# A hybrid of convolution, attention, experts and scans: some scan inputs made by GpSimd, later sums, finer ticks, and the spread in two row groups

## Chip, cores and metric

The kernel runs on one core of a Trainium2 chip, as one program with one launch. The metric is device time in microseconds (us) of a whole execution; lower is better. The engines are TensorE (PE), VectorE (DVE), ScalarE (ACT), GpSimd (POOL) and SyncE (SP), which here issues nearly all DMAs.[...]

## The reference, cut to what matters

Four images of 32 x 32 positions with 256 channels go through four layers. Layer 0 has a state-space scan with 64 states over 512 channels; layer 1 is a grouped convolution block; layer 2 is masked attention and a mixture of 8 experts; layer 3 is a second scan with 16 states, and another mixture of 8 experts. The two scans are what the change is about:

```python
def step(h, inp):                                  # layer 0, N = 64 states
    xt, dtt, Bt, Ct = inp
    dA = jnp.exp(dtt[:, :, None] * A)
    h = dA * h + (dtt * xt)[:, :, None] * Bt[:, None, :]
    y = jnp.einsum('bdn,bn->bd', h, Ct)
    return (h, y)
...
def scan_step(h, inputs):                          # layer 3, N = 16 states
    x_t, dt_t, B_t, C_t = inputs
    A_bar = jnp.exp(dt_t[..., None] * A)
    B_bar = dt_t[..., None] * B_t[:, None, :]
    h_new = A_bar * h + B_bar * x_t[..., None]
    y_t = (h_new * C_t[:, None, :]).sum(axis=-1)
    return (h_new, y_t)
```

There are 1024 time steps for each of 512 channels and 4 images. The mixtures compute, for each expert, `gelu(x @ W1) @ W2` for all tokens, and weight it by the router's value (hidden width 256 in layer 2, 512 in layer 3).

## The kernel before

**Units.** The partitions of a scan hold (channel, state) pairs: 2 channels with 64 states in layer 0, 8 channels with 16 states in layer 3. One such block of 128 x 1024 (float32) is a *unit*. A scan, written (layer, image), has 256 units in layer 0 and 64 in layer 3: for each of four blocks `d` of 128 channels, `c` and `j` choose 32 channels and `i` the group in them. The eight scans, 1280 units, run in the order `SCANS`: (0,0), (0,1), (3,0), (0,2), (3,1), (0,3), (3,2), (3,3).

**One unit, in `scans`.** `load` broadcasts the step widths dt of its channels from DRAM over the states into a tile dA (five buffers): two DMAs of 256 KB in layer 0, eight of 64 KB in layer 3, all issued by SP. `decay` turns dA in place into exp(A dt) on ScalarE. `first` brings dt*x into PSUM (tile ps_rep, two buffers): the program has stored dt*x as three bfloat16 parts (`parts`), which lie in the tile S as 3 x 32 rows, and a product with a table of zeros and ones (`spread`) of 96 rows sums the parts and spreads each channel over its states; there are two products of 512 columns. VectorE multiplies ps_rep by the row B (`rows0`), then runs the scan `tensor_tensor_scan` from dA and ps_rep into h (five buffers). GpSimd multiplies h by C (`rows1`). `pair` then sums over the states on TensorE for two units together into ps_y; after the last pair of a block ScalarE copies ps_y to yo and SP stores it.

**Order within the loop.** At step k the program issues `chunk(k+12)` (the next rows and S where a block begins), `load(k+4)`, `first(k+1)`, `decay(k+2)`, the product by B of unit k; then side work may follow (a `yield`); then the scan of k, the product by C, and on odd k `pair(k-2)`; then side work again.

**Side work and the pacing clock.** All else is written as generators: `front` (layer 0 up to its scan, ending in `steps`, which makes dt and the parts), `middle` (after the scan of layer 0: `back0`, `layer1`, `attention`, `moe`, then `front3`, again with `steps`), and `last` (after the scan of layer 3: `back3`, `moe`). A piece between two yields is a *tick*. `run` decides at each yield of the scan loop whether a tick follows: `Metered` adds a cost for each operation to a clock per engine (`COST`), and up to `TICKS` ticks are added while no engine's clock is past that of vector; the clocks of the other engines are pulled up to at most `LAG` = 4 us behind vector's. A stage starts only when the scan that it needs is done (`STAGES`); a scan starts only when its inputs are stored, else `need` issues side work until they are.

**Ticks that the change touches.** `pipe` runs a list of items through steps, one step behind the other, and yields once per round. In `heads` (attention) a round is the 4 products of values of one block of keys and the 6 products of scores of the next, with two exps. In `moe` a round of kind "h" makes two hidden blocks of 512 columns (ps_h) and evicts the two of the round before by Gelu on ScalarE; a round of kind "o" makes one ps_e, which VectorE adds to tb.

After the last scan the rest of the side work runs alone, and so does `last` of the last image.

Of the kernel before, what the change touches and what calls it, by code (L numbers as in the profile page):

```python
# [16 lines left out]
P = 128  # L17
# [20 lines left out]
SAFE = 40.0  # L38
AHEAD = 12
# [85 lines left out]
class Hybrid:  # L125
# [41 lines left out]
    def pipe(self, items, *steps, cost=1.0):  # L167

        items = list(items)
        for tick in range(len(items) + len(steps) - 1):  # L170
            for s in reversed(range(len(steps))):
                if 0 <= tick - s < len(items):
                    steps[s](items[tick - s])
            yield cost if tick < len(items) else 0.5
# [126 lines left out]
    def scan_setup(self, stage, psum, name, n):  # L301

        nc, pool = self.nc, self.const
        G = P // n
        units = DI // G
        cols = pool.tile([P, units], F32, name="A_" + name)
        flat = self.a[name].rearrange("(u g) n -> u (g n)", g=G)  # L310
        for k in range(0, units, P):
            m = min(P, units - k)
            raw = stage.tile([m, P], F32, name=f"Ar{k}_" + name)
            nc.sync.dma_start(raw, flat[k : k + m, :])
            ps = psum.tile([P, P], F32, tag="pre", name="ps_A")
            nc.tensor.transpose(ps[:, :m], raw, self.ident[:m, :m])
            nc.scalar.activation(cols[:, k : k + m], ps[:, :m], AF.Exp)
        nc.vector.tensor_scalar(cols, cols, -1.0, None, ALU.mult)
        spread = pool.tile([3 * 32, 32 // G, P], BF16, name="spread_" + name)
        for s in range(3):  # L320
            rows = slice(32 * s, 32 * s + 32)
            nc.vector.tensor_copy(
                spread[rows].rearrange("p i (g n) -> p (i g) n", n=n),
                self.ident[rows, rows].unsqueeze(2).to_broadcast([32, 32, n]),
            )
        mine = stage.tile([P, G], F32, name="mine_" + name)
        nc.vector.tensor_reduce(
            mine, self.ident.rearrange("p (g n) -> p g n", n=n), AX.X, ALU.add
        )
        collect = pool.tile([P, 32 // G, 32], F32, name="collect_" + name)  # L330
        nc.gpsimd.memset(collect, 0.0)
        for i in range(32 // G):
            nc.vector.tensor_copy(collect[:, i, G * i : G * i + G], mine)
        return cols, spread, collect

    def scans(self, mp, psum):
# [16 lines left out]
        state = {}  # L353
        y = None

        def chunk(k):
# [17 lines left out]
            S = mp.tile([3 * 32, 4, L], BF16, tag="S", name="S", bufs=2)  # L374
            for s in range(3):
                nc.sync.dma_start(
                    S[32 * s : 32 * s + 32, :, :],
                    self.mem["parts", *scan, d][s].rearrange("(j p) t -> p j t", p=32),
                )
# [16 lines left out]

        def decay(k):
            if k >= len(units):
                return
# [7 lines left out]
        def first(k):  # L407
# [5 lines left out]
            ps = psum.tile([P, L], F32, tag="x", name="ps_rep", bufs=2)  # L413
            for g in range(2):
                cols = slice(g * 512, (g + 1) * 512)
                nc.tensor.matmul(
                    ps[:, cols], lhsT=spread[:, i, :], rhs=chunks[scan, d][:, 2 * c + j, cols],
                    start=True, stop=True,
# [37 lines left out]
        for k in range(len(units) + 4):  # L456
            chunk(k + AHEAD)
            load(k + 4)
            first(k + 1)
            decay(k + 2)  # L460
            if k < len(units):
                a, inp = state.pop(k)
                B, Cm = rows[units[k][0]]
                nc.vector.tensor_tensor(inp, inp, B, ALU.mult)
            yield
            if k < len(units):
                h = mp.tile([P, L], F32, tag="h", name="h", bufs=5)
# [3 lines left out]
            if k % 2 == 1 and 2 <= k < len(units) + 2:  # L471
                pair(k - 2)
# [27 lines left out]
    def run(self):  # L500
# [9 lines left out]
        with tc.tile_pool(name="scan", bufs=1) as mp, tc.tile_pool(  # L510
# [5 lines left out]
            self.nc = Metered(nc, clock)  # L516
# [20 lines left out]
    def steps(self, fp, key, w, src, chunks, bias, u):  # L537
# [3 lines left out]
        for d in range(DC):  # L541
            self.keep(("dt", *key, d), [P, L])
            self.keep(("parts", *key, d), [3, P, L], BF16)
# [27 lines left out]
        def split(item):  # L571
            d, g = item
            r, _, _, x = got[item]
            nc.sync.dma_start(self.mem["dt", *key, d][:, g * 512 : (g + 1) * 512], r)
            X = fp.tile([P, 3, 512], BF16, tag="parts", name="parts", bufs=3)
# [652 lines left out]
    def heads(self, fp, raw, sums, qT, kT, v, maskT, mT, nh, hp):  # L1228
# [41 lines left out]
        yield from self.pipe(range(TB), scores, values, cost=2.6)  # L1270
# [62 lines left out]
    def moe(self, which, b, tb):  # L1333
# [7 lines left out]
        with tc.tile_pool(name=f"m{which}{b}", bufs=1, side="right") as op:  # L1341
# [69 lines left out]
            def one(item):  # L1411
                kind, e, g, i = item
                we1, we2 = weights[e]
                if kind == "h":
# [4 lines left out]
                    got[item] = two = [self.ps("ps_h") for _ in range(2)]  # L1419
                    for s in range(2):  # L1420
                        f = 2 * i + s
                        self.mm(
                            two[s], lambda k: we1[:, k, f * P : (f + 1) * P], xT, 2,
                            slice(g * 512, (g + 1) * 512),
                        )
# [11 lines left out]
            def two(item):  # L1437
                kind, e, g, i = item
                if kind == "h":
                    for s, ps in enumerate(got.pop(item)):  # L1440
                        f = 2 * i + s
                        nc.scalar.activation(
                            hidden_of[e, g][:, f, :], ps, AF.Gelu,
                            bias=b1[:, e * KH + f : e * KH + f + 1],
                        )
# [11 lines left out]
            for n in range(len(blocks) + 1):  # L1457
                if n < len(blocks):
                    items += [("h", *blocks[n], i) for i in range(KH // 2)]
# [271 lines left out]
```

## Time and profile before

Three runs took 7107.39 us in the median (7104.26 to 7117.05). The profiled execution took 7124.43 us; the span from its first to its last instruction is 7122.6 us, with a mean granted TensorE clock of 0.805.

| engine | busy us | share of the span | instructions |
|---|---|---|---|
| PE | 5418.5 | 76% | 20430 |
| DVE | 5222.7 | 73% | 4477 |
| POOL | 3651.6 | 51% | 1801 |
| ACT | 3283.8 | 46% | 4024 |

The 16 DMA engines were busy 49% of the span and moved 939 MB. Busy times are of instructions that compute; instructions that only issue DMAs are not counted, so that SP has no row, and its state is read from the timeline of its issues and from the list of its waits. A row of groups reads: line, engine, operation, output and inputs with shapes, count, busy time, mean duration in ns, and the idle time just before such instructions with what ended it. Where operations are recorded through `Metered` they all carry line 120, so that they are told apart by their tiles: the product by B is the DVE row `ps_rep<-ps_rep,rows`, the scan `h<-dA,ps_rep`, the product by C the POOL row `h<-h,rows`, the spread the PE row `ps_rep<-S,spread`, the sum `ps_y<-h,collect`. Line 391 is the issue of the loads of dA.

### The profile page before, as it was taken

To read this page: it belongs to the slowest core of one execution; us is meant where nothing else is said; L and a number is where in the kernel's file an instruction comes from. 1 tells how busy PE (TensorE), PEld (TensorE's weight loads), DVE (VectorE), ACT (ScalarE), POOL (GpSimd) and SP (SyncE) were. 2 spreads that over 40 slices of the span, in tenths; PEclk is the share of its full clock that TensorE was granted. 3 is DMA by queue.
4 is the path that set the end of the run, shared out by engine and by line. 5 is a ranking of instruction groups with operands and counts; after the bars stand their busy time and mean duration, and the time that the engine had idled before them with its cause. 6 is when DMAs were issued, how large, how long until landed. Compare 5 with 4: busy or idle time off the path is not lost. (4 is left out here: it accounts for less than half of the span.)

```text
span 7122.6 us, 66100 instructions
## 1 busy us (share of the span) xinstructions
PE 5418.5 (76%) x20430; PEld 2202.8 (31%) x20516; DVE 5222.7 (73%) x4477; ACT 3283.8 (46%) x4024; POOL 3651.6 (51%) x1801
## 2 busy tenths in 40 slices
PE   6185876578897557879689668898598677866979
PEld 2020221032242022234235322243254322523556
DVE  2787898887898986789889877888899830237611
ACT  4164665234457324446547334556375332244411
POOL 1287677665557655555756554556656520045300
PEclk8585876579898577979779778888698788877989
DMA  2356666654456565446656654456666620135421
GB/s 82 82 138 165 159 177 165 173 139 112 118 134 172 162 174 130 114 115 174 175 147 165 175 144 113 115 134 175 164 166 165 161 75 1 48 95 158 117 62 33
DMA packets 395052, 939.02 MB, mean 132 GB/s; under 512 B 83268, under 2 KB 165776, under 8 KB 393040
## 3 DMA queue, kind: packets, MB, share of 16 engines
q1 hardware_dynamic: 392512, 932.10, 49.0%
q8 instruction: 172, 2.82, 0.2%
q0 software_dynamic: 2128, 2.13, 0.2%
q14 instruction: 240, 1.97, 0.1%
HBM read 844.17 MB, written 93.95 MB: 132 GB/s over the span
## 5 line engine op out<-in xcount | busy, mean ns | idle before, releaser
L120 POOL TENSOR_TENSOR h<-h,rows 128x1024 f32<-128x1024 f32 x1280 | 3026.2, 2367 | 2198.5 <-DVE h L120 1876.2
L120 DVE TENSOR_TENSOR_SCAN h<-dA,ps_rep 128x1024 f32<-128x1024 f32 x1280 | 2924.9, 2285 | 250.6 <-issue 98.6
L120 DVE TENSOR_TENSOR ps_rep<-ps_rep,rows 128x1024 f32<-128x1024 f32 x1280 | 1552.0, 1212 | 349.2 <-PE ps_rep L120 326.9
L120 ACT ACTIVATE dA<-dA,A_L_conv_A_log 128x1024 f32<-128x1024 f32 x1024 | 1156.7, 1146 | 853.2 <-DMA dA<-dt 767.9
L120 PE MATMUL ps_rep<-S,spread_L_conv_A_log 96*128 96x512 bf16 x2048 | 766.6, 464 | 893.5 <-DVE h L120 718.8
L120 PE MATMUL ps_y<-h,collect_L_conv_A_log 128*32 128x512 f32 x4096 | 767.4, 766 | 91.6 <-POOL h L120 87.7
L120 PEld LDWEIGHTS <-spread_L_conv_A_log 96*128 96x128 bf16 x2048 | 159.2, 103 | 1696.0 <-DVE h L120 1252.3
L120 PE MATMUL ps_h<-xTm,we 128*128 128x512 f32 x1280 | 594.1, 609 | 9.4 <-ACT h_m L120 9.4
L120 PE MATMUL ps_e<-we,h_m 128*128 128x256 f32 x2560 | 590.1, 382 | 10.5 <-ACT h_m L120 8.7
L120 ACT ACTIVATE p<-ps_sc 128x512 f32<-128x512 f32 x512 | 277.8, 594 | 598.1 <-PE ps_sc L120 429.6
L120 ACT ACT_TABLE_LOAD x356 | 456.7, 1283 | 195.5 <-DMA dA<-dt 123.9
L120 ACT ACTIVATE dA<-dA,A_L_attn_A_log 128x1024 f32<-128x1024 f32 x256 | 293.5, 1148 | 514.8 <-DMA dA<-dt 494.9
L120 PEld LDWEIGHTS ps_e<-we,h_m 128*128 128x128 f32 x2560 | 482.9, 190 | 136.6 <-issue 31.5
L120 PE MATMUL ps_at<-p,v 128*32 128x512 f32 x1024 | 366.8, 638 | 61.8 <-ACT p L120 53.3
L120 PE MATMUL ps_rep<-S,spread_L_attn_A_log 96*128 96x512 bf16 x512 | 190.7, 462 | 279.7 <-DVE h L120 236.5
L120 ACT ACTIVATE h_m<-ps_h,cols 128x512 f32<-128x512 f32 x320 | 209.3, 685 | 279.7 <-PE ps_h L120 278.1
L120 PEld LDWEIGHTS ps_h<-xTm,we 128*128 128x128 f32 x1280 | 246.6, 195 | 294.3 <-issue 243.0
L120 DVE SCALAR_TENSOR_TENSOR tb<-ps_e,cw,tb 128x256 f32<-128x256 f32 x448 | 192.4, 473 | 192.9 <-PE ps_e L120 192.4
L120 PE MATMUL ps_sc<-qT,kT 32*128 32x512 f32 x1024 | 310.1, 682 | 0.0
L120 PE MATMUL ps_at<-p,ones 128*32 128x512 f32 x1024 | 285.5, 638 | 0.0
L120 DVE RECIPROCAL sums<-sums 128x512 f32<-128x512 f32 x16 | 53.6, 3353 | 256.6 <-ACT sums L120 256.6
L120 PEld LDWEIGHTS ps_y<-h,collect_L_conv_A_log 128*32 128x32 f32 x4096 | 98.6, 119 | 448.7 <-issue 217.6
(406 smaller groups left out, 5689.3 us busy)
## 6 DMA issues: line engine op xcount, KB each, us to landing
dA<-dt SPq DMA_DIRECT2D x2048, 256.0 KB
dA<-dt SPq DMA_DIRECT2D x2048, 64.0 KB
we<-in_L_ffn_W_dram SPq DMA_DIRECT2D x64, 512.0 KB
parts<-parts SPq DMA_DIRECT2D x64, 384.0 KB
S<-parts SPq DMA_DIRECT2D x96, 256.0 KB
dt<-sp_r SPq DMA_DIRECT2D x64, 256.0 KB
y<-yo SPq DMA_DIRECT2D x128, 128.0 KB
y_back<-y SPq DMA_DIRECT2D x64, 256.0 KB
```

Source lines behind the costliest of these rows:

```text
L120: return got(*args, **kw)
```

## The change

It has four parts.

1. *Inputs by GpSimd.* `steps` also stores dt*x as float32 (`dtu`). At step k, `early(k+5)` looks at the clocks: if gpsimd's is at least `SPARE` = 2.4 us behind vector's, and none of the two units before is one already, unit k+5 is *given*. Its row dtu is broadcast by SP to a new tile inp (two buffers), as dt is to dA, and gpsimd's clock is put 2.4 us forward. `product` has GpSimd multiply inp by B two units ahead; it calls the bare `self.real` and is not metered again. For a given unit `first` has ScalarE write the exp into ps_rep in place of the spread, `decay` does nothing, VectorE does no product by B, and the scan reads ps_rep as its factor and inp as its input.
2. *Sums two units later.* `pair(k-4)` in place of `pair(k-2)`, and h has seven buffers.
3. *Finer ticks.* In `heads` there is a yield between values and scores; in `moe` a round of kind "h" makes one ps_h.
4. *The spread in two row groups.* S holds, in each quarter of 32 partitions, 3 x 8 rows for one `c` and one half of the time steps, with 8 blocks of 512 columns behind each other; it is filled by 12 DMAs of 64 KB rather than 3 of 256 KB. The table `spread` is repeated in all quarters, and the two products of a unit have 24 rows each, in two different quarters.

The diff, cut to its core:

```diff
+SPARE = 2.4
...
-    def pipe(self, items, *steps, cost=1.0):
+    def pipe(self, items, *steps, cost=1.0, cut=False):
...
                 if 0 <= tick - s < len(items):
                     steps[s](items[tick - s])
+                    if cut and s:
+                        yield cost
...
-        spread = pool.tile([3 * 32, 32 // G, P], BF16, name="spread_" + name)
-        for s in range(3):
-            rows = slice(32 * s, 32 * s + 32)
-            nc.vector.tensor_copy(
-                spread[rows].rearrange("p i (g n) -> p (i g) n", n=n),
-                self.ident[rows, rows].unsqueeze(2).to_broadcast([32, 32, n]),
-            )
+        eighth = stage.tile([P, 8], F32, name="eighth_" + name)
+        nc.vector.tensor_reduce(
+            eighth, self.ident.rearrange("p (a c) -> p c a", c=8), AX.X, ALU.add
+        )
+        spread = pool.tile([P, 8 // G, P], BF16, name="spread_" + name)
+        nc.vector.tensor_copy(
+            spread.rearrange("p i (g n) -> p (i g) n", n=n),
+            eighth.unsqueeze(2).to_broadcast([P, 8, n]),
+        )
...
-            S = mp.tile([3 * 32, 4, L], BF16, tag="S", name="S", bufs=2)
-            for s in range(3):
-                nc.sync.dma_start(
-                    S[32 * s : 32 * s + 32, :, :],
-                    self.mem["parts", *scan, d][s].rearrange("(j p) t -> p j t", p=32),
-                )
+            S = mp.tile([P, 8, 512], BF16, tag="S", name="S", bufs=2)
+            for c in range(2):
+                for g in range(2):
+                    for s in range(3):
+                        at = 32 * (2 * c + g) + 8 * s
+                        nc.sync.dma_start(
+                            S[at : at + 8, :, :],
+                            self.mem["parts", *scan, d][
+                                s, 64 * c : 64 * c + 64, g * 512 : (g + 1) * 512
+                            ].rearrange("(k i) t -> i k t", i=8),
+                        )
...
+        def early(k):
+            late = self.clock["vector"] - self.clock["gpsimd"]
+            if k >= len(units) or late < SPARE or max(given, default=-3) > k - 3:
+                return
+            scan, d, c, i, j = units[k]
+            n = self.states[scan[0]]
+            G = P // n
+            inp = mp.tile([P, L], F32, tag="inp", name="inp", bufs=2)
+            for g in range(G):
+                r = 64 * c + 32 * j + G * i + g
+                nc.sync.dma_start(
+                    inp[g * n : (g + 1) * n, :],
+                    self.mem["dtu", *scan, d][r : r + 1, :].to_broadcast([n, L]),
+                )
+            given[k] = inp
+            self.clock["gpsimd"] += SPARE
+
+        def product(k):
+            if k in given:
+                inp = given[k]
+                self.real.gpsimd.tensor_tensor(inp, inp, rows[units[k][0]][0], ALU.mult)
...
         def decay(k):
-            if k >= len(units):
+            if k >= len(units) or k in given:
                 return
...
+            if k in given:
+                col = (d * P + 64 * c + 32 * j) // G + i
+                nc.scalar.activation(
+                    ps, state[k], AF.Exp, scale=self.tables[scan[0]][0][:, col : col + 1]
+                )
+                state[k] = (ps, given[k])
+                return
             for g in range(2):
-                cols = slice(g * 512, (g + 1) * 512)
+                part = slice(32 * (2 * c + g), 32 * (2 * c + g) + 24)
                 nc.tensor.matmul(
-                    ps[:, cols], lhsT=spread[:, i, :], rhs=chunks[scan, d][:, 2 * c + j, cols],
-                    start=True, stop=True,
+                    ps[:, g * 512 : (g + 1) * 512], lhsT=spread[part, i % (8 // G), :],
+                    rhs=chunks[scan, d][part, 4 * j + G * i // 8, :], start=True, stop=True,
                 )
...
-        for k in range(len(units) + 4):
+        for k in range(len(units) + 6):
             chunk(k + AHEAD)
+            early(k + 5)
             load(k + 4)
+            product(k + 2)
             first(k + 1)
             decay(k + 2)
             if k < len(units):
                 a, inp = state.pop(k)
                 B, Cm = rows[units[k][0]]
-                nc.vector.tensor_tensor(inp, inp, B, ALU.mult)
+                if k not in given:
+                    nc.vector.tensor_tensor(inp, inp, B, ALU.mult)
             yield
             if k < len(units):
-                h = mp.tile([P, L], F32, tag="h", name="h", bufs=5)
+                h = mp.tile([P, L], F32, tag="h", name="h", bufs=7)
...
-            if k % 2 == 1 and 2 <= k < len(units) + 2:
-                pair(k - 2)
+            if k % 2 == 1 and 4 <= k < len(units) + 4:
+                pair(k - 4)
...
-            self.nc = Metered(nc, clock)
+            self.real, self.nc = nc, Metered(nc, clock)
...
+            nc.sync.dma_start(self.mem["dtu", *key, d][:, g * 512 : (g + 1) * 512], x)
...
-        yield from self.pipe(range(TB), scores, values, cost=2.6)
+        yield from self.pipe(range(TB), scores, values, cost=1.3, cut=True)
...
-                    got[item] = two = [self.ps("ps_h") for _ in range(2)]
-                    for s in range(2):
-                        f = 2 * i + s
-                        self.mm(
-                            two[s], lambda k: we1[:, k, f * P : (f + 1) * P], xT, 2,
-                            slice(g * 512, (g + 1) * 512),
-                        )
+                    got[item] = ps = self.ps("ps_h")
+                    self.mm(
+                        ps, lambda k: we1[:, k, i * P : (i + 1) * P], xT, 2,
+                        slice(g * 512, (g + 1) * 512),
+                    )
                     return
...
-                    for s, ps in enumerate(got.pop(item)):
-                        f = 2 * i + s
-                        nc.scalar.activation(
-                            hidden_of[e, g][:, f, :], ps, AF.Gelu,
-                            bias=b1[:, e * KH + f : e * KH + f + 1],
-                        )
+                    nc.scalar.activation(
+                        hidden_of[e, g][:, i, :], got.pop(item), AF.Gelu,
+                        bias=b1[:, e * KH + i : e * KH + i + 1],
+                    )
                     return
...
-                    items += [("h", *blocks[n], i) for i in range(KH // 2)]
+                    items += [("h", *blocks[n], i) for i in range(KH)]
```

More of the change, by code (lines that the diff above doesn't have):

```diff
@@ L352, in scans @@
         chunks, rows = {}, {}
-        state = {}
+        state, given = {}, {}
         y = None
@@ L542, in steps @@
             self.keep(("dt", *key, d), [P, L])
+            self.keep(("dtu", *key, d), [P, L])
             self.keep(("parts", *key, d), [3, P, L], BF16)
```

## The prediction

> **What bounds the kernel now.** I read the page first, then busy time by stretches, then the timeline of two quiet stretches, then the waits. Page: the columns are busy time, share and count; then the 40 slices; then the two costly DVE groups.
>
> ```profile
> PE 5418.5 (76%) x20430; PEld 2202.8 (31%) x20516; DVE 5222.7 (73%) x4477; ACT 3283.8 (46%) x4024; POOL 3651.6 (51%) x1801
> DVE  2787898887898986789889877888899830237611
> POOL 1287677665557655555756554556656520045300
> L120 DVE TENSOR_TENSOR_SCAN h<-dA,ps_rep 128x1024 f32<-128x1024 f32 x1280 | 2924.9, 2285 | 250.6 <-issue 98.6
> L120 DVE TENSOR_TENSOR ps_rep<-ps_rep,rows 128x1024 f32<-128x1024 f32 x1280 | 1552.0, 1212 | 349.2 <-PE ps_rep L120 326.9
> ```
>
> From slice 2 to slice 32 (about 310 to 5800 us) VectorE is at 8 to 9 tenths with two operations per unit. Counting ps_rep operations by stretch puts the scans at: (0,0) 310-1380, (0,1) 1380-2555, (3,0) to 2865, (0,2) to 4005, (3,1) to 4325, (0,3) to 5500, (3,2) to 5810; then no scan until 6330, (3,3) to about 6720, and a tail. So 1024 units of layer 0 take some 4560 us, 4.45 each. Timeline near 1320, where no side work runs (start, duration, instruction, idle before):
>
> ```profile
> 1320.02 2.29 DVE L120 TENSOR_TENSOR_SCAN h<-dA,ps_rep 128x1024 f32<-128x1024 f32 x1 [0.19 <-issue]
> 1322.22 1.21 DVE L120 TENSOR_TENSOR ps_rep<-ps_rep,rows 128x1024 f32<-128x1024 f32 x1
> 1323.61 2.29 DVE L120 TENSOR_TENSOR_SCAN h<-dA,ps_rep 128x1024 f32<-128x1024 f32 x1 [0.19 <-issue]
> ```
>
> A unit is 3.59 us, all VectorE. It is not so in layer 3. The timeline of SP (start, length of the run of issues, count), then that of VectorE:
>
> ```profile
> 6379.25 29.88 SPq L391 DMA_DIRECT2D dA<-dt  x64
> ```
>
> ```profile
> 6397.60 2.29 DVE L120 TENSOR_TENSOR_SCAN h<-dA,ps_rep 128x1024 f32<-128x1024 f32 x1 [0.32 <-DMA dA<-dt]
> 6401.40 2.29 DVE L120 TENSOR_TENSOR_SCAN h<-dA,ps_rep 128x1024 f32<-128x1024 f32 x1 [0.40 <-DMA dA<-dt]
> 6405.13 2.29 DVE L120 TENSOR_TENSOR_SCAN h<-dA,ps_rep 128x1024 f32<-128x1024 f32 x1 [0.32 <-DMA dA<-dt]
> ```
>
> There a load is eight DMAs, and 64 issues take 29.88 us: 0.467 each, 3.735 per unit. The scans start 3.7 to 3.8 apart and wait for dA: **SP's issue rate is already the bound.** The tail from 6720 on is PE alone (the chain: ps_h and ps_e in turn, 6.87 and 6.91 us).
>
> **What the Trainium skill says.** "TensorE: Matmul & The Clock Gate", The mechanism: products in distinct row groups run at once. The trace agrees: 32-row bf16 products in pairs (ps_sc<-mT,onesb) keep PE busy 103.1 us for 512, 0.20 each; 128-row ones (maskT) 142.8 for 426, 0.34. "SBUF — State Buffer", SBUF: two separate sides: a DVE operation with two SBUF inputs and a GpSimd operation block each other. It fits: sp_x on DVE takes 1378 ns beside the scans, 1004 in the prologue, 691 at least. The scan has one SBUF and one PSUM input before and after, so it should not lengthen. "ScalarE: Activation LUTs", What ACT_TABLE_LOAD costs: 1283 ns and a drain of some 1380; the trace has 1283 and an activation 0.01 us later, so I charge 1283. No page prices a DMA issue on SP; I take 0.467.
>
> **How many units are given.** By the pacing costs a unit adds 1.27+2.28 = 3.55 us to vector and 2.42 to gpsimd: 1.13 of lag. A given unit books 2.4 and takes 1.27 off vector: 3.67. So 1.13/3.67 = 0.31 of units, one in three at most; less where side work is POOL's (steps: four operations of 1.27 us per item). I take 0.30: 307 in layer 0, 77 in layer 3. Bounds 0.10 and 0.33.
>
> **Part by part.**
> 1. VectorE: a given unit loses 1.21 us and the gap before its scan, 1.31 in all. 307 x 1.31 = **-402** in layer 0 if VectorE stays the bound everywhere. POOL gains 384 x 2.37 = 910 us. Three units with one given cost 9.5 us on POOL and 3x3.59-1.31 = 9.5 on VectorE: balanced, POOL just fits.
> 2. What takes it back in layer 0:
>  - Attention, about 225 units: PE runs gapless there, two units in 8.23 us. A spread pair costs 0.53 of it; as two row groups I take 0.26 (bounds 0.20 and 0.53). PE saves 0.53-0.7x0.26 = 0.35 per unit, not 0.39: +9. The later sums remove up to 0.42 per two units of PE waiting for POOL's h; I leave that as reserve.
>  - Expert blocks, about 250 units. Today ACT loads the gelu table, evicts two ps_h, loads exp. With one ps_h per tick an exp falls between them in some seven of ten cases. 356 loads on this line become some 540: +184 x 1.283 = 236 us of ACT, nearly 0.95 per unit. ACT is busy 133 of 200 us there (2.7 per unit of 4.1); 3.65 fills it. Queued behind it: decay's exps and PE's buffers. I give these units no gain: +98. Bounds 0 and +160.
>  - Fronts, 187 units: POOL is busy 76%; 0.2 of the units rather than 0.3: +24.
>  - S by 12 DMAs rather than 3 per chunk, 9 x 0.45 = 4 us of SP ahead of the dA loads. After the burst of rows and S at 1334 a scan waited only 0.19 us, so slack is nearly used up: 16 chunks x 2 us = +32.
>  - Two-input DVE side operations behind a busier POOL (51% to some 65%): about 300 operations, 0.1 us more each: +30.
>  Layer 0: -402+9+98+24+32+30 = **-209**.
> 3. Layer 3: 77 given units x 8 broadcasts x 0.467 = +288 us of SP, and 16 chunks x 4 = +65 for S: 353. SP has waits of its own to swallow some. In 2560-2860 it waited 16.1 us for yo and 13.9 for scans, some 50 of 300 with all; in (3,3) 23 and 11. The later sums make yo ready before SP comes to it, so I let three fifths, 210 us, be swallowed and VectorE's 77 x 1.31 = 100 be worth nothing, as it no longer bounds. That leaves about **+140**. Bounds -100 and +350.
> 4. DMA traffic: 384 x 0.52 MB = +200 MB on 939. Without side work the share is 0.66 at 169 GB/s; at 3.2 us a unit with 1.3 loads it would be about 0.9. Nearly full, not over: 0, bounds 0 and +60.
> 5. Priced at nothing: the given exp into PSUM waits for scan k-1 but has unit k to run in (1.15 of 2.3 us; without that cover each would cost 1.15). dtu stores are 64 issues, covered by waits of the fronts, +29 if not. Sums and stores later: two units, 7 us, per scan, under side work. New spread table: under 2 us before the scan.
> 6. The spread itself in quiet and mixed stretches, about 600 us less PE busy, hides under VectorE, which has only 327 us of waits for ps_rep; finer ticks shorten PE's bursts from 2.9 to some 1.4 us and could recover a third of it. Taken as **-30**.
> 7. Tail and the stretch 5810-6330: same PE work in the same order, 0.
>
> Sum: -209+140-30 = -99. The profiled execution took 7124.43 us (span 7122.6, 1.8 around it), 17 above the median 7107.39; applied to the median: 7008, say **7010**.
>
> **Rivals.**
> - **SP decides (slower).** The eight broadcasts of a given unit are not swallowed: all 353 us stand, and layer 0 gives 209+30, less DMA waits of 0 to 60. 7107+353-239 = 7221, or 7200 with a little absorbed. It decides once more than 239 us of new SP time reaches the scans. For it: SP at its rate in (3,3). Against: (3,0) to (3,2) run at 4.8 us a unit, above 3.735.
> - **VectorE's gain stands whole.** ACT's loads hide, PE's relief shows, SP's extra time fits in the waits: 7107-402-100+60, near 6665; with three fifths of it 6800. For it: VectorE at 85% over the scans with only 349 us of idle before products. Against: SP above.
> - **Few units are given.** If side work keeps gpsimd's clock up, 0.1 of the units: a third of each effect, but all extra S issues and table loads: about 7090.
>
> **How the numbers follow.** Forecast 0.45 (own range 6930 to 7085), whole gain 0.23, SP decides 0.26, few given 0.06. About 0.2% (14 us) is what a measurement can tell from no change. Faster: all of the second, most of the first and some of the last, 0.67; same 0.05; slower 0.28. Range 6790 to 7200: it leaves out about one in ten of the whole-gain cases' far end and one in ten on the slow side.
>
> **What would show it.** About 384 POOL products of 2.37 us on inp and as many exps into ps_rep; ps_rep products near 900 on DVE, still 1.21, the scan still 2.29. In the stretch without side work a mean unit of 3.2. In layer 3 SP gapless, with scans waiting for dA or inp and 5 us or more per unit. ACT_TABLE_LOAD on this line well above 356. PE spread pairs starting together. Wrong if layer-3 scans become shorter than about 310 us each, if expert stretches gain as much as quiet ones, if the scan lengthens beside POOL, or if POOL's products wait for inp and hold up h.

## The result, and the profile after

The changed kernel takes 7385.88 us in the median of four runs (7376.91 to 7402.99) against 7112.22 for the kernel before on the same chip: a ratio of 1.0387, 95% interval 1.0362 to 1.0411. That is 275 us slower, where 7010 us and a gain were forecast. The profiled span is 7401.2 us. First the page, busy time and two of the rows of slices, then its groups:

```profile
PE 5124.4 (69%) x19896; PEld 2130.1 (29%) x19896; DVE 4897.8 (66%) x4165; ACT 3346.9 (45%) x4082; POOL 4352.7 (59%) x2111
...
DVE  2778788877788765788888556788795601146411
...
POOL 1288888767678755667877546768685500055300
```

```profile
L121 DVE TENSOR_TENSOR_SCAN h<-dA,ps_rep 128x1024 f32<-128x1024 f32 x970 | 2216.2, 2285 | 396.0 <-ACT dA L121 210.8
L121 DVE TENSOR_TENSOR ps_rep<-ps_rep,rows 128x1024 f32<-128x1024 f32 x970 | 1176.7, 1213 | 330.3 <-PE ps_rep L121 329.3
...
L121 DVE TENSOR_TENSOR_SCAN h<-ps_rep,inp 128x1024 f32<-128x1024 f32 x310 | 706.3, 2278 | 298.8 <-ACT ps_rep L121 236.0
L431 POOL TENSOR_TENSOR inp<-inp,rows 128x1024 f32<-128x1024 f32 x310 | 730.3, 2356 | 104.3 <-DMA dA<-dt 60.7
```

The work moved as planned: 310 units are given, VectorE is busy 325 us less, and each operation of VectorE is as long as before. But the idle time ahead of the scans grew from 250.6 to 396.0 + 298.8 us. VectorE's list of waits (what it waited for, total us, times, longest) says for whom:

```profile
DVE ps_rep L121 <- PE ps_rep L121: 329.3, 153, 14.1
...
DVE h L121 <- ACT ps_rep L121: 236.0, 97, 14.8
DVE h L121 <- ACT dA L121: 210.8, 58, 35.0
...
DVE h L121 <- DMA dA<-dt: 89.8, 34, 16.9
```

The wait for PE's spread is as it was (326.9), the other three are new or larger. They are exps that come late, and an exp of dA waits for its loads in turn.

Cut at the first and last scan instruction of each scan, with the stretch without scans set apart (it lies inside (3,2), twelve units before its end, where the program issues side work until the inputs of (3,3) are stored), the spans divide so (us):

| kernel | start | scans of layer 0 | (3,0) | (3,1) | (3,2) | (3,3) | stretch | tail |
|---|---|---|---|---|---|---|---|---|
| before | 313 | 4513 | 344 | 346 | 329 | 315 | 541 | 413 |
| after | 323 | 4448 | 395 | 412 | 378 | 378 | 613 | 438 |

Layer 0 gained 65 us, though VectorE is busy some 260 us less in its scans. The scans of layer 3 lost 229 us, the stretch and the tail 97, the start 10.

### The profile page after: what moved, and what is told of

It reads as the page before. It is cut to its first block, busy times and chain, and to the rows that moved or that the text cites. A ratio compares the mean times of both kernels' runs of the same rounds, so it can differ in the third digit from the quotient of the medians.

```text
span 7401.2 us, 67114 instructions
## 1 busy us (share of the span) xinstructions
PE 5124.4 (69%) x19896; PEld 2130.1 (29%) x19896; DVE 4897.8 (66%) x4165; ACT 3346.9 (45%) x4082; POOL 4352.7 (59%) x2111
## 5 line engine op out<-in xcount | busy, mean ns | idle before, releaser
L121 DVE TENSOR_TENSOR_SCAN h<-dA,ps_rep 128x1024 f32<-128x1024 f32 x970 | 2216.2, 2285 | 396.0 <-ACT dA L121 210.8
L121 DVE TENSOR_TENSOR ps_rep<-ps_rep,rows 128x1024 f32<-128x1024 f32 x970 | 1176.7, 1213 | 330.3 <-PE ps_rep L121 329.3
L121 ACT ACTIVATE dA<-dA,A_L_conv_A_log 128x1024 f32<-128x1024 f32 x780 | 881.1, 1143 | 505.0 <-DMA dA<-dt 457.1
L121 PE MATMUL ps_rep<-S,spread_L_conv_A_log 24*128 24x512 bf16 x1560 | 371.4, 468 | 1057.9 <-DVE h L121 901.6
L121 DVE TENSOR_TENSOR_SCAN h<-ps_rep,inp 128x1024 f32<-128x1024 f32 x310 | 706.3, 2278 | 298.8 <-ACT ps_rep L121 236.0
L431 POOL TENSOR_TENSOR inp<-inp,rows 128x1024 f32<-128x1024 f32 x310 | 730.3, 2356 | 104.3 <-DMA dA<-dt 60.7
L121 ACT ACT_TABLE_LOAD x414 | 531.2, 1283 | 304.4 <-DMA dA<-dt 249.3
L121 PEld LDWEIGHTS <-spread_L_conv_A_log 24*128 24x128 bf16 x1560 | 80.4, 94 | 1691.0 <-DVE h L121 1085.0
L121 ACT ACTIVATE dA<-dA,A_L_attn_A_log 128x1024 f32<-128x1024 f32 x190 | 217.5, 1147 | 643.4 <-DMA dA<-dt 536.3
L121 ACT ACTIVATE ps_rep<-dA,A_L_conv_A_log 128x1024 f32<-128x1024 f32 x244 | 272.7, 1118 | 281.6 <-DVE h L121 148.0
L121 PE MATMUL ps_rep<-S,spread_L_attn_A_log 24*128 24x512 bf16 x380 | 94.1, 486 | 377.4 <-DVE h L121 366.2
```

The costliest lines, as they stand in the source:

```text
L121: return got(*args, **kw)
L431: self.real.gpsimd.tensor_tensor(inp, inp, rows[units[k][0]][0], ALU.mult)
```

## The experiments

In the table us is (ratio - 1) x 7112; the columns after it divide the span of the profiled execution as above, layer 3 without the stretch. Each run was compared with runs of the kernel before on the same chip. Most intervals reach 0.1 to 0.2% either way, 7 to 14 us, and the columns are of one execution each, so that smaller differences between two rows say little. To *book* is to add a cost to the pacing clock of an engine; the *pace* is how much side work these clocks let in beside a unit.

| label | kernel | ratio (interval) | us | layer 0 | layer 3 | stretch | tail |
|---|---|---|---|---|---|---|---|
| before | | 1 | 0 | 4513 | 1334 | 541 | 413 |
| after | the whole change | 1.0387 (1.0362 to 1.0411) | +275 | 4448 | 1563 | 613 | 438 |
| a_no3 | after, none given in layer 3 | 1.0029 (1.0015 to 1.0043) | +21 | 4422 | 1440 | 534 | 411 |
| a_none | after, none given | 1.0339 (1.0317 to 1.0361) | +241 | 4660 | 1419 | 530 | 414 |
| b_spread | before + spread | 1.0318 (1.0296 to 1.0340) | +226 | 4655 | 1409 | 529 | 403 |
| b_sums | before + later sums | 1.0012 (1.0005 to 1.0019) | +9 | 4511 | 1316 | 540 | 420 |
| b_heads | before + attention ticks | 0.9926 (0.9903 to 0.9948) | -53 | 4454 | 1320 | 534 | 413 |
| b_moe | before + expert ticks | 0.9958 (0.9944 to 0.9973) | -30 | 4491 | 1325 | 541 | 417 |
| b_s12 | before + S by twelve DMAs | 1.0203 (1.0181 to 1.0225) | +144 | 4562 | 1417 | 541 | 413 |
| b_half | before + spread booked at half | 1.0109 (1.0092 to 1.0126) | +78 | 4597 | 1336 | 531 | 404 |
| b_spread_full | before + spread, booked in full | 1.0206 (1.0189 to 1.0223) | +147 | 4533 | 1440 | 533 | 413 |
| b_one | before, one DMA per load | 1.9056 (1.9017 to 1.9094) | | 10894 | 1401 | 541 | 413 |
| a_one | after, one DMA per load | 2.2911 | | 13475 | 1400 | 616 | 438 |
| best1 | after, none given in layer 3, old spread | 0.9796 (0.9779 to 0.9814) | -145 | 4294 | 1300 | 635 | 423 |
| best3 | best1, removed product booked | 1.0037 (1.0024 to 1.0050) | +26 | 4506 | 1339 | 541 | 419 |
| best2 | a_no3, spread booked in full | 1.0030 (1.0017 to 1.0042) | +21 | 4342 | 1381 | 637 | 421 |
| a_book | after, removed product booked | 1.0554 (1.0537 to 1.0572) | +394 | 4569 | 1636 | 534 | 406 |
| g0 | before + given units of layer 0 | 0.9780 (0.9756 to 0.9803) | -156 | 4298 | 1296 | 629 | 413 |
| g0_book | g0, removed work booked | 0.9898 (0.9877 to 0.9918) | -73 | 4425 | 1352 | 535 | 414 |
| b_pace | before, booked as g0 | 0.9952 (0.9934 to 0.9970) | -34 | 4427 | 1288 | 623 | 413 |

The mean granted TensorE clock is 0.805 before and 0.784 after. That this is the cause is not what the runs show: the same products ps_h of the expert blocks take 609 ns in the mean before, 623 after, and 605 in b_half, whose time is 78 us longer all the same.

### Which part costs: given units in each layer

```diff
 # a_no3
-            if k >= len(units) or late < SPARE or ...
+            if k >= len(units) or units[k][0][0] == 3 or late < SPARE or ...
 # a_none
-SPARE = 2.4
+SPARE = 1.0e9
```

> The changed kernel, but no unit of layer 3 is given (244 given units remain, all in layer 0). Theory SP (the eight extra issues of a given unit of layer 3 and the finer S loads overload SP's queue): 66 x 8 x 0.467 = 247 us of issue go, the four layer-3 scans lose 150 to 250 of the 302 us that they gained, so 7140 to 7240. Theory ACT (a given unit gains nothing anywhere, because its exponential comes late in ScalarE's queue and VectorE waits for it): only the 37 to 20 us of such waits per layer-3 scan go, 7270 to 7310. Theory ticks (finer ticks cost): no change, 7370 to 7390.

> The changed kernel with no given unit at all; later sums, finer ticks and the new spread stay. Theory SP: as without those of layer 3, and in addition layer 0 gives its gain of 65 us back: 7200 to 7300. Theory ACT: given units are a net loss in both layers, so below the run without those of layer 3: 7110 to 7170. Theory ticks: what remains of the loss is ticks and S loads, 7300 or more.

Taking the 66 given units out of layer 3 brings 254 us, about as much as their issues take on SP, 66 x 8 x 0.467 = 247. But the columns say that it is not all SP: 123 us go in the scans of layer 3 (half of SP's time), 106 in the stretch and the tail, 26 in layer 0. Two causes, which two other runs part. In a_one SP's issues are fewer and the booking is the same: the scans of layer 3 drop from 1563 to 1400, stretch and tail stay. In a_book the booking is raised again: stretch and tail go back to 534 and 406, and the scans stand 196 us above those of a_no3, for 71 given units and 265 us of SP. **So at about the pace of before, given units of layer 3 make its scans longer by three quarters of the SP time that they add, net of the product that VectorE is spared; and where a given unit books less, side work is put off past the last scans as well, which here buys nothing.** SP is not alone in it: in layer 3 VectorE waits 112 us for the given exps after, 75 in a_book and still 76 in a_one, which is about what the 66 removed products save (66 x 1.21 = 80). The timeline of SP in the kernel after, some units into scan (3,3) (start, length of the run of issues, line, count), and VectorE's beside it:

```profile
6631.54 14.09 SPq L387 DMA_DIRECT2D S<-parts  x12
6645.99 4.25 SPq L421 DMA_DIRECT2D inp<-dtu  x8
6650.28 29.76 SPq L404 DMA_DIRECT2D dA<-dt  x64
```

```profile
6620.94 1.21 DVE L121 TENSOR_TENSOR ps_rep<-ps_rep,rows 128x1024 f32<-128x1024 f32 x1
6657.20 2.29 DVE L121 TENSOR_TENSOR_SCAN h<-dA,ps_rep 128x1024 f32<-128x1024 f32 x1 [35.05 <-ACT dA L121]
6660.95 2.29 DVE L121 TENSOR_TENSOR_SCAN h<-ps_rep,inp 128x1024 f32<-128x1024 f32 x1 [1.46 <-ACT ps_rep L121]
```

The wait is put down to ScalarE, but its exp waited for dA:

```profile
6656.02 1.15 ACT L121 ACTIVATE dA<-dA,A_L_attn_A_log 128x1024 f32<-128x1024 f32 x1 [37.31 <-DMA dA<-dt]
```

And dA's eight issues stand behind twelve of S and eight of inp in SP's order. Only a part of this wait is new. In the kernel before, at the same place behind the loads of y_back and gate_back, the loads of dA come ahead of those of S, and VectorE waits too:

```profile
6436.36 2.29 DVE L120 TENSOR_TENSOR_SCAN h<-dA,ps_rep 128x1024 f32<-128x1024 f32 x1 [20.50 <-DMA dA<-dt]
```

In layer 0 given units are worth 220 us here (a_none against a_no3); the last group shows what that is made of.

### Each other part alone

Each is the hunks of that part from the diff, applied to the kernel before.

> The kernel before with the new spread alone (24 rows in two row groups, S by 12 DMAs). Without any given unit the other three parts cost 3.4% together, 245 us. Theory S (the finer S loads and the lower booked cost of the spread, which lets more side work in per unit, cost it): 7200 or more. Theory ticks (finer ticks cost it): 7080 to 7120, with PE busy some 400 us less and nothing gained, since VectorE is the bound.

> The kernel before with the later sums alone (pair two units later, seven buffers for h). All theories: 7080 to 7120; it takes away waits of PE for POOL (88 and 27 us) that mostly hide.

> The kernel before with the finer ticks of attention alone. Theory ticks: at most a third of the loss, as no table load is added: 7110 to 7180. Theory S: 7080 to 7120, shorter PE bursts ahead of ps_rep.

> The kernel before with the finer ticks of the expert blocks alone. Theory ticks: the gelu and exp tables alternate more often (414 loads on the line rather than 356) and each added pair delays exps and evictions: 7180 to 7330. Theory S: 7100 to 7130.

The spread, which I had priced as a small gain with a small cost in S, is the second large loss. The later sums bring nothing (+9). Finer ticks gain, and the expert ticks do so although the table loads came nearly as the prediction had them (some 540; the expectation for this run, with 414, had the count of the kernel after), in the group of b_moe:

```profile
L120 ACT ACT_TABLE_LOAD x506 | 649.2, 1283 | 167.2 <-DMA dA<-dt 115.5
```

150 more loads than the 356 of before, 192 us of ScalarE, and the kernel is faster: ScalarE, busy for 49% of the span of b_moe, has room for them.

### The spread taken apart

```diff
 # b_s12: the old tile and table, its rows by twelve DMAs of 8 (src: those rows of parts)
-                nc.sync.dma_start(S[32 * s : 32 * s + 32, :, :], src)
+                for q in range(0, 32, 8):
+                    nc.sync.dma_start(S[32 * s + q : 32 * s + q + 8, :, :], src[q : q + 8])
 # b_half: the old spread, only its price on the pacing clock
-    return us / 2 if lhsT.shape[0] <= 32 else us
+    return us / 2 if lhsT.shape[0] <= 32 or lhsT.shape[0] == 96 else us
 # b_spread_full: the new spread at the old price
+    return us / 2 if lhsT.shape[0] <= 32 and lhsT.shape[0] != 24 else us
```

> The kernel before with the same tile S filled by 12 DMAs of 8 rows in place of 3 of 32. Theory booked: 64 us of extra SP time over 32 chunks, some of it swallowed: 7110 to 7160. Theory S: 7250 or more.

> The kernel before with the old spread unchanged, only booked at half price on the pacing clock. Theory booked: most of the 222 us appears although no instruction is new, 7230 to 7400 (more than the new spread, since PE really spends the full price). Theory S: no change, 7100 to 7130.

> The kernel before with the new spread, its two products booked on the pacing clock at the full price as before (0.47 us a unit) and not at half. The new spread alone costs 222 us. Theory booked (the lower booked price packs more side ticks into a unit, and their chains of dependent work stall VectorE's queue): most of the 222 us goes, 7110 to 7190. Theory S (the 12 short DMAs for S hold up the loads behind them): 7290 to 7340.

It adds up: 144 for the loads and 78 for the booking are 222, and the whole spread is 226; with the full booking only the loads' 147 remain. What TensorE saves is therefore worth nothing that these intervals, some 15 us either way, can show. **The loads**: SP's timeline in the kernel before, then in b_s12, while the first block of (3,0) runs:

```profile
2578.97 1.32 SPq L376 DMA_DIRECT2D S<-parts  x3
```

```profile
2613.30 5.96 SPq L377 DMA_DIRECT2D S<-parts  x12
```

A block costs 4.64 us more, 32 blocks 148, practically all of the loss. Layer 3 takes 83 of it, 5.2 per block, layer 0 49, 3.1 per block, the start 9. S itself does not land too late: in layer 3 VectorE waits no longer for TensorE's spread than before (143 us in b_s12, 149 before). But its waits for dA grow there from 48 to 91 us, more than half of the 83.

**The booking**: TensorE's spread at half the price lets more side ticks in beside each unit. The row of products by B, of b_half and then of b_spread_full (the last figures are VectorE's idle time before them):

```profile
L120 DVE TENSOR_TENSOR ps_rep<-ps_rep,rows 128x1024 f32<-128x1024 f32 x1280 | 1554.4, 1214 | 400.3 <-PE ps_rep L120 399.0
```

```profile
L120 DVE TENSOR_TENSOR ps_rep<-ps_rep,rows 128x1024 f32<-128x1024 f32 x1280 | 1552.3, 1213 | 339.7 <-PE ps_rep L120 333.2
```

The cost lies in layer 0 alone (4513 to 4597). Only the booking differs, and denser side work puts more TensorE work ahead of a unit's spread: 72 us more of this wait than the 326.9 of before, where full booking leaves 6.

### One DMA per load

Shortened, with `rows` for the rows of one unit:

```diff
-            for g in range(G): nc.sync.dma_start(a[g * n : (g + 1) * n, :], row.to_broadcast([n, L]))
+            nc.sync.dma_start(a, rows.unsqueeze(1).to_broadcast([G, n, L]))
```

> The kernel before, with each load of dA as one DMA in place of two or eight. Theory SP: SP was the bound only in part of the layer-3 scans; the 26 us of waits for dA in (3,3) and a little elsewhere go: 7050 to 7090. Theories ACT and ticks: no change from before, 7105 to 7120.

> The changed kernel, with each load of dA and of inp as one DMA (the broadcast of all its channels in one access) in place of two or eight; the same bytes. Theory SP: SP's time per layer-3 unit falls from 3.7 us to about 0.5, the 302 us of layer 3 go and more, since also the kernel before was near SP's rate there: 7000 to 7100. Theory ACT: layer 3 keeps its waits for the exponential: 7250 to 7330. Theory ticks: no change.

Both fail in layer 0, where one load is then two rows by 64 states. The issues of dA in b_one (ns, least/median/most):

```profile
L390 SPq DMA_DIRECT2D dA<-dt x1280: 475/9202/16991, 304.2 to 13156.8; - x183
```

DMA moved 69 GB/s in the mean of the whole run, and each layer-0 scan took some 2715 us. The Trainium skill, "DMA: Bandwidth & Descriptors", Why a DMA increments its semaphore by 16 and not by 1, says that a DMA uses the largest number of engines, up to 16, that divides the slowest dimension on both of its sides; that dimension is now 2 in layer 0. The trace agrees: the share of the 16 engines that is busy, in tenths by slice, is mostly 1 in b_one (0.17 between 400 and 3000 us, 2.7 engines, where before has 0.61 between 400 and 1300):

```profile
DMA  1112111112111111151111211151111211140341
```

Layer 3, where it is 8, can still be read: SP's issues in (3,0) fall from 298 us after to 109 in a_one, and the scans of layer 3 lose 163 us with them, to 19 us less than a_none's, which points to SP. In b_one the scans of layer 3 are 67 us longer than before, though SP's issues take a third of the time (78 instead of 235 us in (3,0)): there the transfers themselves seem to set the pace, which no run tried by itself.

### What a given unit of layer 0 is worth

> The changed kernel with no given unit in layer 3 and with the old spread; given units in layer 0, later sums and finer ticks stay. If the parts add up: 7139 without layer 3's given units, less the 222 us of the spread: 6890 to 6950, faster than both kernels.

best1 beats both kernels with 6973.06 us, but its parts promise more: -156 (g0, run later), +9, -53 and -30 are -230, and it has -145. Its stretch without scans is 635 us long rather than 541: side work is left over. So three runs booked the removed work again.

```diff
 # best3, a_book (best2: the price of b_spread_full)
+                else:
+                    self.clock["vector"] += 1.27
```

> The kernel after without given units in layer 3 and with the old spread and its three loads of S, as in the run before this, and besides the pacing clock of VectorE is raised by 1.27 us for each given unit (the time of the product by B that VectorE no longer does), so that the side work is paced as if it still did. Nothing of the computation changes. Theory A (with fewer booked microseconds on VectorE a given unit admits less side work, the side work is left over at the end of the scans, and that is what the separate gains lose when they are put together): the stretch without scans before the last scan but one shrinks from 635 us to some 540, the last store of the third batch element comes before the end of scan (0,3) again, and the time is about 6973 - 95 = 6880 us, ratio 0.967. Theory B (the loss lies in the scans, where more side work per unit makes new waits): the stretch shrinks, but the layer-0 scans lengthen by as much, and the time stays within 20 us of 6973, ratio 0.980.

> The kernel after without given units in layer 3, and with the new spread booked on the pacing clock at the full price of the old one, its twelve loads of S kept. Nothing of the computation changes. Theory A (the halved booking costs 78 us beside the loads, in the whole as alone): 7139 - 78 = about 7060 us, ratio 0.992. Theory B (in the whole the halved booking is what keeps the side work under the scans, since given units leave less of it there): 7140 to 7200 us, ratio 1.003 to 1.012, with a stretch without scans of over 600 us in place of 534.

> The kernel after with one change: the pacing clock of VectorE is raised by 1.27 us for each given unit. Nothing of the computation changes. Theory A (the parts tried alone leave about 95 us of the loss unexplained, and side work left over after the scans is most of it): the stretch without scans shrinks from 613 us to some 540 and the time is about 7310 us, ratio 1.028. Theory B (the remainder lies in the scans themselves): within 20 us of 7386, ratio 1.039.

**My theory fell.** The stretch came back as it said, 635 to 541 us and 613 to 534. But the kernels became slower, by 171 and 119 us in the table; the layer-0 scans of best3 take 4506 us against 4294 in best1 and 4513 before. In best2 more booking on TensorE did the opposite, 534 to 637 us, and the time stayed. So side work under the scans is not free, and what is left over is not lost. That made it open whether the gain of given units is the removed product at all. Three more runs and the kernel before make a two by two:

```diff
 # g0: part 1 alone, layer 0 alone.   g0_book:
+                else:
+                    self.clock["vector"] += 1.27
+                    self.clock["tensor"] += 0.47
 # b_pace: units picked by g0's rule, nothing moved (the spread of a picked unit likewise unbooked)
+                vector = self.real.vector if k in given else nc.vector
-                nc.vector.tensor_tensor(inp, inp, B, ALU.mult)
+                vector.tensor_tensor(inp, inp, B, ALU.mult)
```

> The kernel before with the given units of layer 0 as the one part of the change (old spread, old sums, old ticks, none given in layer 3). Nothing of the computation changes. A given unit loses the product by B on VectorE, and with it 1.27 us on VectorE's pacing clock and 0.47 us on TensorE's. Theory A (the removed product is the gain, some 220 us as measured between the kernel after without any given unit and the one with those of layer 0): about 6890 us, ratio 0.969. Theory B (most of those 220 us came from the lowered booking, which took back what finer ticks and the halved spread had put under the scans too densely; without these there is less to take back): 6980 to 7060 us, ratio 0.982 to 0.993.

> The run g0 with the removed work booked all the same: 1.27 us on VectorE's pacing clock and 0.47 us on TensorE's for each given unit, so that the side work is paced as in the kernel before while VectorE is free of some 250 products. Nothing of the computation changes. Theory A (the product's 1.18 us x 250 are worth their time on VectorE): 6830 to 6930 us, ratio 0.96 to 0.975. Theory B (at that pace the side work's waits and not VectorE's own work set the length of a layer-0 scan, as the run with finer ticks and this booking suggests, whose layer-0 scans sum to 4509 us against 4512 in the kernel before): 7090 to 7150 us, ratio 0.997 to 1.005.

> The kernel before with only the booking of g0: by the same rule units of layer 0 are picked, and for these the product by B and the spread are issued as ever but not put on the pacing clocks, and GpSimd's clock is raised by 2.4 us. No product is moved and nothing is loaded in place of it; nothing of the computation changes. Theory A (the gain is the removed product): slower than before by the side work left over after the scans, some 7110 to 7210 us, ratio 1.00 to 1.014. Theory B (the gain is the pace): faster than before by over 50 us, below 7060 us, ratio below 0.993, and g0 lies about as far below g0_book.

| | booked | not booked |
|---|---|---|
| product on VectorE | 0 (before) | -34 (b_pace) |
| product on POOL | -73 (g0_book) | -156 (g0) |
| layer-0 scans, us | 4513; 4425 | 4427; 4298 |

Neither theory holds alone: the removed product, net of the loads and the exp that it takes, is worth 73 us at an unchanged pace and 122 at the lower one; the lower pace is worth 34 to 83. (By its clocks g0_book gives 259 units and g0 244, so that the 73 are for somewhat more products.) The two rows of products show why (g0, then g0_book):

```profile
L121 DVE TENSOR_TENSOR ps_rep<-ps_rep,rows 128x1024 f32<-128x1024 f32 x1036 | 1257.2, 1213 | 363.5 <-PE ps_rep L121 341.9
...
L121 DVE TENSOR_TENSOR_SCAN h<-ps_rep,inp 128x1024 f32<-128x1024 f32 x244 | 554.7, 2274 | 134.2 <-ACT ps_rep L121 119.6
```

```profile
L121 DVE TENSOR_TENSOR ps_rep<-ps_rep,rows 128x1024 f32<-128x1024 f32 x1021 | 1239.6, 1214 | 458.8 <-PE ps_rep L121 439.5
```

At the old pace some 100 us more than in g0 go into waiting for the spread, and 113 more than the 326.9 of before. That fits: VectorE is ready sooner and TensorE, busy with the same side work per unit, isn't. With the lower pace the scans gain, and the side work left over makes the stretch 629 us instead of 535.

## Why the prediction was wrong

Forecast was -99 and came +275, 374 apart. By place: layer 0 -209 forecast and -65 measured; layer 3 +140 and +229; stretch and tail 0 and +97; the spread's -30 that didn't come, and 10 at the start. Three steps carry most of it. Given units of layer 0 gain 156 us where step 1 put 402. Those of layer 3 cost 254 where step 3 let 115 of their 288 us of SP stand. The spread costs 226 alone where step 6 put -30 and the loads of S were charged with 58 (32 in layer 0, two fifths of 65 in layer 3).

By part the measured sum is: given units of layer 0 -156, of layer 3 +254, spread +226, sums +9, ticks -83: +250 of the +275. The 25 left over are two interactions of opposite sign: on top of given units the finer ticks and sums bring nothing (85 us lost), and in that company the spread costs 166 (a_no3 against best1), not 226.

- **How many are given**: 310, not 384: 244 in layer 0 (0.24 of the units) and 66 in layer 3. Within the bounds.
- **Step 1, -402 us: mis-sized.** It nearly holds where VectorE has no other work: the units 89 to 121 of (0,0), around 720 to 830 us, take 3.63 us each before and 3.31 in g0, where 10 of these 33 are given: 0.32 less, with 10/33 x 1.21 = 0.37 removed. Over the whole, 266 us of VectorE's work went (5222.7 to 4956.5 in g0) and 156 came out. "If VectorE stays the bound everywhere" was the condition that failed.
- **Step 5, the given exp into PSUM priced at nothing: wrong.** VectorE waits 236.0 us for it after (112 of them in layer 3) and 119.6 in g0. VectorE and then ScalarE in the kernel after:

```profile
798.02 2.29 DVE L121 TENSOR_TENSOR_SCAN h<-dA,ps_rep 128x1024 f32<-128x1024 f32 x1
803.40 2.29 DVE L121 TENSOR_TENSOR_SCAN h<-ps_rep,inp 128x1024 f32<-128x1024 f32 x1 [3.09 <-ACT ps_rep L121]
```

```profile
798.17 0.69 ACT L121 ACTIVATE u<-ps_cv,cols 128x512 f32<-128x512 f32 x1
798.76 0.68 ACT L121 ACTIVATE pad<-ps_in,cols 128x512 f32<-128x512 f32 x1
799.33 1.56 ACT L121 ACTIVATE diag<-ident,cols 128x128 f32<-128x128 f32 x5
800.90 1.28 ACT L121 ACT_TABLE_LOAD   x1
802.20 1.12 ACT L121 ACTIVATE ps_rep<-dA,A_L_conv_A_log 128x1024 f32<-128x1024 f32 x1
```

  The step asked only whether PSUM is free in time. The exp is issued with `first(k+1)`, one unit ahead where `decay` is two, and stands in ScalarE's order behind 2.9 us of side work and a table load. The load takes the 1283 ns that the Trainium skill states ("ScalarE: Activation LUTs", What ACT_TABLE_LOAD costs); the exp starts 0.02 us behind it, so that the 1380 ns of drain that the page adds do not show here. No run issued this exp earlier, so what that would bring is open.
- **Step 2, expert ticks +98: wrong in sign.** Alone they bring -30. The loads were counted nearly right for these ticks alone (506) and not for the whole (414, not 540); the conclusion was wrong, as ScalarE had room. Why finer ticks bring nothing beside given units no run settles, and the small terms of this step (+9, +24, +30) no run reads apart.
- **Steps 2 and 3, S by twelve DMAs: mis-sized.** The 4.64 us per block are near the 4 estimated; I let slack take half of it in layer 0 and three fifths in layer 3. It took a third in layer 0 and nothing in layer 3.
- **Step 3, +140 for layer 3: wrong in its main term.** Right: SP's added issues lengthen the scans, at 0.467 each. Wrong: "three fifths swallowed". SP's added time is 247 + 16 x 4.64 = 321 us, and the scans are 229 longer: under a third was swallowed. The 23 and 11 us for which I had seen SP wait in (3,3) were no measure of what it can absorb. Nor is SP's rate "the bound" over a whole scan, as one gapless run of 64 issues made me say: the 539 issues in (3,0) come to 252 of 344 us before and 710 to 332 of 395 after, and added issues reach the scans all the same. And two fifths of what given units of layer 3 cost, 106 of 254 us, was not in the step at all: a given unit lowers the booking whether or not it gains, which accounts for the 97 us of stretch and tail. The rival that SP decides was right in sign; at 7200 to 7221 it had the spread and this for nothing, and 239 us from layer 0.
- **Step 4, DMA**: 1118 MB moved, near the forecast 939 + 200; the wait for dA grew from 52.7 to 89.8 us.
- **Step 6, the spread -30: wrong.** Two 24-row products do run side by side, as the Trainium skill says ("TensorE: Matmul & The Clock Gate", The mechanism). The rows of before and after (busy, mean ns):

```profile
L120 PE MATMUL ps_rep<-S,spread_L_conv_A_log 96*128 96x512 bf16 x2048 | 766.6, 464 | 893.5 <-DVE h L120 718.8
```

```profile
L121 PE MATMUL ps_rep<-S,spread_L_conv_A_log 24*128 24x512 bf16 x1560 | 371.4, 468 | 1057.9 <-DVE h L121 901.6
```

  That is 0.238 us of busy time per product rather than 0.374, for layer 0. It is worth nothing in time, since it is VectorE that a spread waits for (901.6 us), and I did not see that the pacing clock believes the saving and fills it with side work: 78 us.
- **Step 7, 0: wrong**, +72 for the stretch and +25 for the tail, as said under step 3. The stretch also lies elsewhere than the prediction read it, inside (3,2) ahead of its last twelve units, and the scans of layer 3 took 344, 346, 329 and 315 us before, 5.4 to 4.9 a unit rather than 4.8.
- **Right**: the scan's duration (2285 ns, 2278 with inp), as the Trainium skill's "SBUF — State Buffer", SBUF: two separate sides, suggests for one SBUF and one PSUM input; POOL's product (2356 ns) and its room: scans waited for inp 29.8 us in all.

Best of all kernels run are g0 with 6960.90 and best1 with 6973.06 us, which their intervals do not tell apart.

## What to carry to other kernels

A queue need not be full for an added issue to be paid in full: SP's issues came to 252 of 344 us in (3,0), and the splitting of S still reached the scans of layer 3 whole. Take slack off only for waits that lie between the added issue and the one that is late next. An operation that is moved to another engine takes a place in that engine's order, so ask how far ahead of its reader it is issued, compared with the one that it replaces, and what stands before it. Where side work is admitted by booked costs, a cheaper operation also changes the pace: test the booking apart from the operation, as a two by two.

## What was not expected of the hardware

- A DMA that broadcasts two rows over 64 partitions each in one instruction took SP 9.9 us in the median of (0,1) (9.2 over all loads of b_one), where a single row's issue takes some 0.5 (322 us for 613 issues in (0,0) before) and eight rows over 16 partitions each take 0.575 in (3,0).
- Twelve issues of 64 KB for S take SP 5.96 us and three of 256 KB 1.32: 0.50 and 0.44 each. For these loads the count of DMAs sets SP's time, not their bytes.
